# A graph layer on one core: the sums of a turn put between two first layers, and VectorE's two-input work cut into operations of 128 columns

## The chip, the cores and the metric

One core of a Trainium2 chip runs the whole layer. The metric is device time in microseconds (us), the median of three runs. "PE" is TensorE, "PEld" its weight loads, "DVE" VectorE, "ACT" ScalarE, "POOL" GpSimd and "SP" SyncE. All arithmetic is float32. The profiler writes each float32 matmul as two records, so counts of matmuls below are counts of records.

## The reference

6,250 nodes with 256 features, 206,250 edges sorted by destination, 65 numbers for each edge (the first is a polarity, the others features).

```python
h = jnp.maximum(_layernorm(x, axis=-1), 0.0)
polarity = jnp.clip(edge_attr[:, 0:1], 0.0, 1.0)
raw = edge_attr[:, 1:]
e = jax.nn.relu(raw @ W_e1.T + b_e1) @ W_e2.T + b_e2
edge_emb = (e * (polarity + 0.01)) @ W_le.T + b_le
msg = jax.nn.relu(h[src] + edge_emb)
aggr = jax.ops.segment_sum(msg, dst, num_segments=6250)
g = (h + aggr) @ W_g1.T + b_g1
gn = (g - mean(g)) * rsqrt(var(g) + 1e-5) * ln_g + ln_b
return x + jax.nn.relu(gn) @ W_g2.T + b_g2
```

W_e2 and W_le are multiplied together once (`wc_s`), so an edge costs two matrix products: the first layer (64 to 256) and the product with `wc_s` (256 to 256).

## The kernel before, in words

**Tiling.** The sorted edges are cut into blocks of 512 (four tiles of 128). Two blocks make a pair (202 pairs, index `q`); half a block, 256 edges, makes a unit (806 units, index `u`). Six blocks make a group (68 groups, index `g`); each group's sums stand in one PSUM tile `pd`, in four strips of 32 rows. 49 windows of 128 nodes finish the layer. Seven PSUM buffers `pz` go round for everything else; a new tile waits until the tile seven before it has been read.

**A unit.** `edge_part(u)` puts 8 matmul records of 256 columns on PE (L266) and one addition of 512 columns on DVE (L271), which reads PSUM and so frees the buffer. Later `whole(u)` multiplies the message by the polarity and adds the gathered rows of h (L551, two DVE operations of 256 columns, one per half of `hg[u]`, each with two tensors in SBUF and a per-row scalar), and ACT takes the maximum with 0 (L556). The rows of h are gathered by POOL, two indirect DMAs for a unit (L528), into 16 buffers `hg`. The gather for a unit is issued behind a matmul of a certain earlier unit (`last_z`) and needs a buffer that the sums have freed. `whole` trails `edge_part` by 22 units at the start and by 1 at the end.

**A turn.** Every eighth unit, for pairs 6 to 195, `turn_of` (L281) works for two pairs at once: `first_layer(q + 2)`, `first_layer(q + 3)`, then `sums`, which is `add_pairs` (L587), then the loads of two further pairs on SP. A first layer is 8 matmul records of 512 columns into four PSUM buffers (L243); ACT empties three of these (L251) and DVE one (L248). The sums are 32 records (L566), one-hot matrices `sel` by finished messages `hg`; when a group is complete ACT copies it out (L577). Engines take their instructions in the order in which this code issues them.

**What else DVE does.** `select(g)` (L536) makes the one-hot tiles of a group, one comparison of 768 columns (L541), with two tensors in SBUF. For each window `ready` (L636) multiplies and then adds statistics to the transposed x in `hT` (L639, two operations of 256 columns), and `offset` (L204) adds a bias to the rows of x (L205, 256 columns). These too read two tensors in SBUF each, and have no per-row scalar. They are called through `at(unit, fn)` and `due()` (L693): each unit takes at most one such call from the list, none in the turn's unit and the one ahead of it.

Of the kernel before, what the change touches and what calls it, by code (L numbers as in the profile page):

```python
# [17 lines left out]
P = 128  # L18
# [10 lines left out]
S = 4  # L29
L = 6  # L30
# [63 lines left out]
def gnn_kernel(ctx: ExitStack, tc: tile.TileContext, x, src_c, dst_c, dst_r, pol_c, raw_t, w_e1t, w_e2,  # L94
# [16 lines left out]

    ident = const.tile([P, P], F32, name="ident")
    eps_t = const.tile([P, 1], F32, name="eps_t")
    we1_s = const.tile([P, D], F32, name="we1_s")
    wc_s = const.tile([P, 2, D], F32, name="wc_s")
    bc_s = const.tile([P, 2, D], F32, name="bc_s")
# [27 lines left out]
    def finish_nodes(nd, ps, w, n):  # L144

        r = w * P

        def turn(a):
            pt = ps()
            for c in range(2):  # L150
                nc.tensor.transpose(pt[:, 0, c * P:c * P + n], a[:n, c * P:(c + 1) * P], ident[:n, :n])
            aT = nd.tile([P, 2, P], F32, name="aT")
            if n == P:
                nc.scalar.activation(aT, pt[:, 0, :].rearrange("p (c n) -> p c n", c=2), AF.Copy)
            else:
                for c in range(2):
                    nc.scalar.activation(aT[:, c, :n], pt[:, 0, c * P:c * P + n], AF.Copy)
            return aT

        def first(aT, bias_by_pe=False):  # L160
            ph = ps()
            if bias_by_pe:
                nc.tensor.matmul(ph[:n, 0, :], ones[0:1, :n], bg1_b[0:1], start=True, stop=False)
            for c in range(2):
                nc.tensor.matmul(ph[:n, 0, :], aT[:, c, :n], wg1_s[:, c, :], start=c == 0 and not bias_by_pe, stop=c == 1)  # L165
            hs = nd.tile([P, D], F32, name="hs")
            if bias_by_pe:
                hb = ph[:, 0, :]
            else:
                hb = hs  # L170
                nc.vector.tensor_add(hs[:n], ph[:n, 0, :], bg1_b[:n])
            mv = row_stats(nd, n, 1, lambda i: hb[:n])
            rs = nd.tile([P, 1], F32, name="rs1")
            one_over_std(rs[:n], mv, n)
            nc.vector.tensor_scalar(hs[:n], hb[:n], mv[:n, 0, 0:1], rs[:n], op0=ALU.subtract, op1=ALU.mult)
            return hs

        def second(hs):
            pt = ps()
            for c in range(2):  # L180
                nc.tensor.transpose(pt[:, 0, c * P:c * P + n], hs[:n, c * P:(c + 1) * P], ident[:n, :n])  # L181
            nT = nd.tile([P, 2, P], F32, name="nT")
            for c in range(2):
                nc.scalar.activation(nT[:, c, :n], pt[:, 0, c * P:c * P + n], AF.Relu, bias=lnb_s[:, c:c + 1],  # L184
                                     scale=lng_s[:, c:c + 1])
            return nT

        def third(nT, xt):
            po = ps()
            for c in range(2):  # L190
                nc.tensor.matmul(po[:n, 0, :], nT[:, c, :n], wg2_s[:, c, :], start=c == 0, stop=c == 1)  # L191
            ot = nd.tile([P, D], F32, name="ot")
            nc.vector.tensor_add(ot[:n], po[:n, 0, :], xt[:n])
            for i, (a, b) in enumerate(spread_out(n)):
                eng = nc.scalar if i else nc.sync
                eng.dma_start(out=out[bass.ds(r + a, b - a), :], in_=ot[a:b])

        def load_x():
            xt = nd.tile([P, D], F32, name="xt3")
            for a, b in spread_out(n):  # L200
                nc.sync.dma_start(out=xt[a:b], in_=x[bass.ds(r + a, b - a), :])
            return xt

        def offset(xt):  # L204
            nc.vector.tensor_add(xt[:n], xt[:n], bg2_b[:n])  # L205

        return turn, first, second, third, load_x, offset

# [3 lines left out]
    with fast:  # L212
# [68 lines left out]
        def turn_of(q):  # L281


            if not by_two(q):
                if q + 2 < NP:
                    first_layer(q + 2)
                sums(q == NP - 1)
                load_pair(q + 4)
            elif q % 2 == 0:
                first_layer(q + 2)  # L290
                first_layer(q + 3)
                sums(False)
                load_pair(q + 4)
                load_pair(q + 5)

# [4 lines left out]
                turn_of(u // 4)  # L300

        nc.vector.memset(eps_t, EPS)
        nc.vector.memset(ones, 1.0)
        nc.vector.memset(rs_s, 0.0)
        nc.vector.memset(nm_s, 0.0)
# [207 lines left out]
        with tc.tile_pool(name="hg", bufs=HG) as hg_p, tc.tile_pool(name="ms", bufs=5) as ms_p, \  # L513
# [21 lines left out]

            def select(g):  # L536

                n = len(blocks_of(g)) * S
                t = g * L * S
                sel[g] = sel_p.tile([P, L * S, W], F32, name="sel")  # L540
                nc.vector.tensor_tensor(  # L541
                    sel[g][:, :n, :], iota_w.rearrange("p (o w) -> p o w", o=1).to_broadcast([P, n, W]),
                    rel[:, t:t + n].rearrange("p (t o) -> p t o", o=1).to_broadcast([P, n, W]), ALU.is_equal)

            def whole(u):

                m = msg.pop(u)
                if plain(u):
                    nc.vector.tensor_add(m, m, bc_s)
                for i in range(2):  # L550
                    nc.vector.scalar_tensor_tensor(hg[u][:, i, :], m[:, i, :], pol_s[:, 2 * u + i:2 * u + i + 1],  # L551
                                                   hg[u][:, i, :], op0=ALU.mult, op1=ALU.add)
                    if u == NU - 1:
                        nc.scalar.activation(hg[u][:, i, :], hg[u][:, i, :], AF.Relu)
                if u < NU - 1:
                    nc.scalar.activation(hg[u], hg[u], AF.Relu)  # L556

            def add_up(b):

                g = group_of(b)  # L560
                k = b - g * L
                if k == 0:
                    acc[g] = pd[:, g % 2, :] if g < NG - 1 else ps()[:, 0, :]
                for j in range(S):
                    m = hg[2 * b + j // 2]
                    nc.tensor.matmul(acc[g][j * W:(j + 1) * W, :], sel[g][:, k * S + j, :], m[:, j % 2, :],  # L566
                                     start=k == 0, stop=b == blocks_of(g)[-1])
                hg.pop(2 * b)
                hg.pop(2 * b + 1)
                return g if b == blocks_of(g)[-1] else None  # L570
# [16 lines left out]
            def add_pairs(last=False):  # L587
# [3 lines left out]
                while summed < NP and min(4 * summed + 4, NU) < made + last:  # L591
                    for b in (2 * summed, 2 * summed + 1):
                        if b < NB:
                            whole_groups.append(add_up(b))
                            if b % L == 0 and group_of(b) + 2 < NG:
                                at(now + 2, lambda g=group_of(b) + 2: select(g))
                    summed += 1

                for g in whole_groups:
# [3 lines left out]
            todo = {}  # L603
            now = 0
            late = {}
            ending = {-2: [], -1: []}

            def at(u, fn):
# [2 lines left out]
            def node_work(w, spread_now=False):  # L611
# [7 lines left out]
                def spread():  # L619
# [7 lines left out]
                    for g in gs:  # L627
# [1 line left out]
                        nc.vector.tensor_scalar(s2, iota_p, rowid[:, g:g + 1], float(-w * P), op0=ALU.subtract,  # L629
                                                op1=ALU.is_equal)  # L630
                        box["sel2"].append(s2)
                    at(now + 3, lambda: ready(0))
                    at(now + 4, lambda: ready(1))
                    at(now + 5, lambda: offset(box["xt"]))

                def ready(i):  # L636

                    hT, st = box["hT"], box["st"]
                    nc.vector.tensor_tensor(hT[:, :, :n], hT[:, :, :n], st[:, i:i + 1, :n].to_broadcast([P, 2, n]),  # L639
                                            (ALU.mult, ALU.add)[i])  # L640

                def sums_of(part):

# [56 lines left out]

            gathers(HG)
            sums = add_pairs
            for i, fn in ((0, first_rows), (1, rows_of_edges), (3, lambda: select(0)), (5, row_numbers), (6, stats_out),
                          (7, lambda: select(1)), (8, node_weights)):
                at(LEAD + i, fn)
            for i, fn in enumerate((by_group(0, ALU.max), by_group(1, ALU.min), by_row(0, ALU.max), by_row(1, ALU.min),
                                    verdict, count, total)):
# [2 lines left out]
            for u in range(LEAD, NU):  # L710
# [8 lines left out]
                else:  # L719
                    gathers(4 * summed + HG - 4 + (u - TURN) % 4 + 1, last_z)  # L720

                while made < u + 1 - max(LEAST, LEAD - u // SHRINK) - (by_two(u // 4) and (u + 1) % 8 == TURN):
                    whole(made)
                    made += 1
                due()
                if u == NU - 24:
                    for w in range(NW):
                        if groups_of(w)[-1] == NG - 1:
                            late[w] = node_work(w, True)
                if u == LEAD + 60:  # L730
                    flag = nc.values_load(bad_i[0:1, 0:1], min_val=0, max_val=3 * P)
            while todo:
                now = min(todo)
                for fn in todo.pop(now):
                    fn()
            before, last = ending[-2], ending[-1]
            for sums_of, halves_out, rows_of, one, two, three, gs in before:
                rows_of()
# [28 lines left out]
def any_order(tc, dram, v):  # L767
# [7 lines left out]
    with tc.tile_pool(name="sc", bufs=1) as sc, tc.tile_pool(name="sk", bufs=2) as sk, \  # L775
# [78 lines left out]
        def nodes(w, n):  # L854
# [1 line left out]
            nc.sync.dma_start(out=ac[:n], in_=acc_d[bass.ds(w * P, n), :])  # L856
            turn, one, two, three, load_x, offset = v["finish_nodes"](sk, lambda: sp1.tile([P, 1, D], F32, name="ps_a"), w, n)
            xt = load_x()
            offset(xt)
            three(two(one(turn(ac))), xt)  # L860

        with tc.For_i(0, full, 1) as w:
# [65 lines left out]
```

## Time and profile before

| what | us |
|---|---|
| median of three runs (2186.34 to 2188.13) | 2187.48 |
| time of the profiled execution | 2189.23 |
| its span, first to last instruction | 2187.4 |
| PE busy in the span | 2169.5 |
| POOL busy | 1648.4 |
| DVE busy | 1604.4 |
| ACT busy | 960.8 |

The page of the profile gives busy time for each engine, the costliest groups of instructions by source line with the mean duration of one, and the idle time ahead of them with what ended it. A busy PE says little, since matmuls overlap and their ends are modelled. What counts is the distance from one start to the next. For POOL the page counts the indirect DMA instruction alone as busy; what lies between two of them stands as idle time. The mean granted TensorE clock was 0.997.

### The profile page before, as it was taken

To read this page: it belongs to the slowest core of one execution; us is meant where nothing else is said; L and a number is where in the kernel's file an instruction comes from. 1 tells how busy PE (TensorE), PEld (TensorE's weight loads), DVE (VectorE), ACT (ScalarE), POOL (GpSimd) and SP (SyncE) were. 2 spreads that over 40 slices of the span, in tenths; PEclk is the share of its full clock that TensorE was granted. 3 is DMA by queue.
4 is the path that set the end of the run, shared out by engine and by line. 5 is a ranking of instruction groups with operands and counts; after the bars stand their busy time and mean duration, and the time that the engine had idled before them with its cause. 6 is when DMAs were issued, how large, how long until landed. Compare 5 with 4: busy or idle time off the path is not lost.

```text
span 2187.4 us, 34907 instructions
## 1 busy us (share of the span) xinstructions
PE 2169.5 (99%) x12382; PEld 1625.1 (74%) x12382; DVE 1604.4 (73%) x3470; ACT 960.8 (44%) x1701; POOL 1648.4 (75%) x1675
## 2 busy tenths in 40 slices
PE   9999999999999999999999999999999999999998
PEld 6677777777777777777677777777777777777776
DVE  7787777777777777777677777777777767777675
ACT  7444444444444444444444444343444444444443
POOL 5777777777777777777777777777777777777775
PEclk9999999999999999999999999999999999999999
DMA  9544445454545454545544445445444445454543
GB/s 313 159 134 134 138 126 157 130 149 122 151 126 155 119 155 125 151 123 151 142 122 139 142 139 151 129 121 156 139 131 128 143 130 153 131 146 130 150 123 89
DMA packets 156075, 309.17 MB, mean 141 GB/s; under 512 B 33183, under 2 KB 77944, under 8 KB 155896
## 3 DMA queue, kind: packets, MB, share of 16 engines
q0 software_dynamic: 77376, 211.39, 33.7%
q1 hardware_dynamic: 77364, 92.23, 13.7%
q10 hardware_dynamic: 1156, 3.28, 0.4%
q8 instruction: 98, 1.61, 0.3%
q14 instruction: 81, 0.66, 0.1%
HBM read 293.92 MB, written 12.85 MB: 140 GB/s over the span
## 4 chain that ended last, share of the span: by engine, by line
PE 92%; DMA 3%; POOL 2%; DVE 2%; issue 1%; ACT 1%; ACTq 0%; DVEq 0%; POOLq 0%
PE pz L266 60%; PE pz L243 16%; PE pd L566 9%; PE pz L664 3%; DMA hg<-hb_d,src_s 3%; PE pz L165 2%; PE pz L191 2%; POOL hg L528 2%; DVE msg L271 1%; PE pz L181 1%; DMA xt<-in_x_dram 0%; ACT xt L366 0%; DVE hg L551 0%; DVE st L136 0%; PE pz L307 0%
## 5 line engine op out<-in xcount | busy, mean ns | idle before, releaser
L528 POOL DMA_INDIRECT hg<-hb_d,src_s x1612 | 1611.2, 999 | 495.5 <-issue 355.3
L266 PE MATMUL pz<-wc_s,e 128*128 128x256 f32 x6448 | 1452.3, 381 | 1.3 <-ACT msg L269 1.3
L266 PEld LDWEIGHTS pz<-wc_s,e 128*128 128x128 f32 x6448 | 1208.7, 190 | 203.8 <-issue 28.8
L556 ACT ACTIVATE hg<-hg 128x512 f32<-128x512 f32 x805 | 500.5, 629 | 1048.0 <-DVE hg L551 1030.5
L551 DVE SCALAR_TENSOR_TENSOR hg<-msg,pol_s,hg 128x256 f32<-128x256 f32 x1612 | 711.3, 478 | 153.3 <-DMA hg<-hb_d,src_s 148.9
L271 DVE TENSOR_TENSOR msg<-pz,bc_s 128x512 f32<-128x512 f32 x799 | 542.9, 685 | 224.0 <-PE pz L266 223.0
L243 PE MATMUL pz<-raw,we_s 64*128 64x512 f32 x1612 | 402.8, 608 | 6.9 <-DVE msg L271 6.6
L251 ACT ACTIVATE e<-pz,vecs 128x512 f32<-128x512 f32 x605 | 361.8, 692 | 88.0 <-PE pz L243 86.9
L243 PEld LDWEIGHTS pz<-raw,we_s 64*128 64x128 f32 x1612 | 160.2, 186 | 195.6 <-issue 127.2
L248 DVE TENSOR_SCALAR e<-pz,vecs 128x512 f32<-128x512 f32 x201 | 150.5, 749 | 164.6 <-PE pz L243 164.6
L566 PE MATMUL pd<-hg,sel 128*32 128x256 f32 x3216 | 196.9, 386 | 0.0
L566 PEld LDWEIGHTS pd<-hg,sel 128*32 128x32 f32 x3216 | 95.0, 110 | 129.3 <-issue 77.6
L664 PEld LDWEIGHTS pz<-s,ms 128*128 128x128 f32 x548 | 68.7, 192 | 3.1 <-issue 0.4
L664 PE MATMUL pz<-s,ms 128*128 128x128 f32 x548 | 69.3, 275 | 0.1
L541 DVE TENSOR_TENSOR sel<-iota_w,rel 128x768 f32<-128x768 f32 x68 | 63.9, 940 | 0.0
L370 POOL TENSOR_TENSOR hb<-xt,rows_b 128x256 f32<-128x256 f32 (+1 forms) x49 | 34.1, 728 | 24.2 <-ACT xt L366 18.2
L191 PE MATMUL pz<-wg_s,nT 128*128 128x256 f32 (+1 forms) x196 | 50.6, 380 | 0.6 <-ACT nT L184 0.6
L165 PE MATMUL pz<-wg_s,hT 128*128 128x256 f32 (+1 forms) x196 | 50.5, 380 | 0.0
L577 ACT ACTIVATE ms<-pd 128x256 f32<-128x256 f32 x66 | 25.4, 384 | 51.5 <-PE pd L566 51.5
L191 PEld LDWEIGHTS pz<-wg_s,nT 128*128 128x128 f32 (+1 forms) x196 | 37.1, 190 | 5.9 <-ACT nT L184 0.8
L165 PEld LDWEIGHTS pz<-wg_s,hT 128*128 128x128 f32 (+1 forms) x196 | 37.0, 190 | 5.7 <-issue 0.3
L639 DVE TENSOR_TENSOR hT<-hT,stb 128x256 f32<-128x256 f32 x98 | 40.8, 417 | 0.0
(90 smaller groups left out, 378.2 us busy)
## 6 DMA issues: line engine op xcount, KB each, us to landing
raw<-in_raw_t_dram SPq DMA_DIRECT2D x202, 256.0 KB
hg<-hb_d,src_s POOLq DMA_INDIRECT x1612
stb<-st_d SPq DMA_DIRECT2D x49, 128.0 KB
hb_d<-hb SPq DMA_DIRECT2D x12, 512.0 KB
xt<-in_x_dram SPq DMA_DIRECT2D x48, 128.0 KB
hT<-in_x_t_dram SPq DMA_DIRECT2D x48, 128.0 KB
out_dram<-ot SPq DMA_DIRECT2D x48, 128.0 KB
xt<-in_x_dram SPq DMA_DIRECT2D x11, 512.0 KB
```

Of the source, the lines that this page charges most:

```text
L165: nc.tensor.matmul(ph[:n, 0, :], aT[:, c, :n], wg1_s[:, c, :], start=c == 0 and not bias_by_pe, stop=c == 1)
L191: nc.tensor.matmul(po[:n, 0, :], nT[:, c, :n], wg2_s[:, c, :], start=c == 0, stop=c == 1)
L243: nc.tensor.matmul(pe[s, c], we1_s[s * F:(s + 1) * F, c * P:(c + 1) * P], raw[q][s * F:(s + 1) * F, :], start=True, stop=True)
L248: nc.vector.tensor_scalar(e1[b][:, c, :], pe[s, c], be1_s[:, c:c + 1], 0.0, op0=ALU.add, op1=ALU.max)
L251: nc.scalar.activation(e1[b][:, c, :], pe[s, c], AF.Relu, bias=be1_s[:, c:c + 1])
L266: last_z = nc.tensor.matmul(pz[:, i, :], e1[b][:, c, k:k + P], wc_s[:, c, :], start=c == 0, stop=c == 1)
L271: nc.vector.tensor_add(msg[u], pz, bc_s)
L528: g = nc.gpsimd.indirect_dma_start(out=hg[u][:, i, :], out_offset=None, in_=hb_d, in_offset=bass.IndirectOffsetOnAxis(ap=src_s[:, 2 * u + ...
L551: nc.vector.scalar_tensor_tensor(hg[u][:, i, :], m[:, i, :], pol_s[:, 2 * u + i:2 * u + i + 1], hg[u][:, i, :], op0=ALU.mult, op1=ALU.add)
L556: nc.scalar.activation(hg[u], hg[u], AF.Relu)
L566: nc.tensor.matmul(acc[g][j * W:(j + 1) * W, :], sel[g][:, k * S + j, :], m[:, j % 2, :], start=k == 0, stop=b == blocks_of(g)[-1])
L664: nc.tensor.matmul(pa[:, c, :n], ms[g][:, c * P:(c + 1) * P], box["sel2"][i][:, :n], start=i == 0, stop=i == len(gs) - 1)
```

## The change

It does four things. The sums of a turn are issued between its two first layers. Each product of `whole` is issued as two operations of 128 columns. The one-hot comparison is issued block by block (six pieces of 128 columns), and `ready` and `offset` in halves of 128 columns; these become `scalar_tensor_tensor` with a per-row scalar `zero_c` that is added first (a column of zeros, written once at the start). And they no longer go through `due()`: `piece()` issues one of them in each unit ahead of the products, those of a window first (`steps`), otherwise the next one-hot piece (`rest`), and a second one when more than six one-hot pieces are left. Before a group's first sums, pieces of that group still left would be issued at once.

```diff
@@ turn_of
             elif q % 2 == 0:
                 first_layer(q + 2)
+                sums(False)
                 first_layer(q + 3)
-                sums(False)
                 load_pair(q + 4)
                 load_pair(q + 5)
@@ offset
-        def offset(xt):
-            nc.vector.tensor_add(xt[:n], xt[:n], bg2_b[:n])
+        def offset(xt, c):
+            h = slice(c * P, (c + 1) * P)
+            nc.vector.scalar_tensor_tensor(xt[:n, h], xt[:n, h], zero_c[:n], bg2_b[:n, h], op0=ALU.add, op1=ALU.add)
@@ select
-                n = len(blocks_of(g)) * S
-                t = g * L * S
-                sel[g] = sel_p.tile([P, L * S, W], F32, name="sel")
-                nc.vector.tensor_tensor(
-                    sel[g][:, :n, :], iota_w.rearrange("p (o w) -> p o w", o=1).to_broadcast([P, n, W]),
-                    rel[:, t:t + n].rearrange("p (t o) -> p t o", o=1).to_broadcast([P, n, W]), ALU.is_equal)
+                return [(g, lambda k=k: rows_of_block(g, k)) for k in range(len(blocks_of(g)))]
+
+            def rows_of_block(g, k):
+                t = (g * L + k) * S
+                if k == 0:
+                    sel[g] = sel_p.tile([P, L * S, W], F32, name="sel")
+                nc.vector.scalar_tensor_tensor(
+                    sel[g][:, k * S:(k + 1) * S, :], iota_w.rearrange("p (o w) -> p o w", o=1).to_broadcast([P, S, W]),
+                    zero_c, rel[:, t:t + S].rearrange("p (t o) -> p t o", o=1).to_broadcast([P, S, W]), op0=ALU.add,
+                    op1=ALU.is_equal)
+
+            def piece():
+                if steps and steps[0][0] <= now:
+                    steps.popleft()[1]()
+                elif rest:
+                    rest.popleft()[1]()
@@ whole
                 for i in range(2):
-                    nc.vector.scalar_tensor_tensor(hg[u][:, i, :], m[:, i, :], pol_s[:, 2 * u + i:2 * u + i + 1],
-                                                   hg[u][:, i, :], op0=ALU.mult, op1=ALU.add)
+                    for c in range(2):
+                        h = slice(c * P, (c + 1) * P)
+                        nc.vector.scalar_tensor_tensor(hg[u][:, i, h], m[:, i, h], pol_s[:, 2 * u + i:2 * u + i + 1],
+                                                       hg[u][:, i, h], op0=ALU.mult, op1=ALU.add)
@@ add_up, add_pairs
+                    while rest and rest[0][0] <= g:
+                        rest.popleft()[1]()
...
-                                at(now + 2, lambda g=group_of(b) + 2: select(g))
+                                rest.extend(select(group_of(b) + 2))
@@ node_work
-                    at(now + 3, lambda: ready(0))
-                    at(now + 4, lambda: ready(1))
-                    at(now + 5, lambda: offset(box["xt"]))
+                    steps.extend((now + 3, lambda i=i, c=c: ready(i, c)) for i in range(2) for c in range(2))
+                    steps.extend((now + 3, lambda c=c: offset(box["xt"], c)) for c in range(2))
...
-                def ready(i):
+                def ready(i, c):
-                    nc.vector.tensor_tensor(hT[:, :, :n], hT[:, :, :n], st[:, i:i + 1, :n].to_broadcast([P, 2, n]),
-                                            (ALU.mult, ALU.add)[i])
+                    nc.vector.scalar_tensor_tensor(hT[:, c, :n], hT[:, c, :n], zero_c, st[:, i, :n], op0=ALU.add,
+                                                   op1=(ALU.mult, ALU.add)[i])
@@ main loop
+                piece()
                 while made < u + 1 - max(LEAST, LEAD - u // SHRINK) - (by_two(u // 4) and (u + 1) % 8 == TURN):
                     whole(made)
                     made += 1
                 due()
+                if len(rest) > 6:
+                    piece()
```

More of the change, by code (lines that the diff above doesn't have):

```diff
@@ L113, in gnn_kernel @@
     eps_t = const.tile([P, 1], F32, name="eps_t")
+    zero_c = const.tile([P, 1], F32, name="zero_c")
     we1_s = const.tile([P, D], F32, name="we1_s")
@@ L302, in gnn_kernel @@
         nc.vector.memset(eps_t, EPS)
+        nc.vector.memset(zero_c, 0.0)
         nc.vector.memset(ones, 1.0)
@@ L605, in gnn_kernel @@
             late = {}
+            steps = deque()
+            rest = deque()
             ending = {-2: [], -1: []}
@@ L702, in gnn_kernel @@
             sums = add_pairs
-            for i, fn in ((0, first_rows), (1, rows_of_edges), (3, lambda: select(0)), (5, row_numbers), (6, stats_out),
-                          (7, lambda: select(1)), (8, node_weights)):
+            for i, fn in ((0, first_rows), (1, rows_of_edges), (3, lambda: rest.extend(select(0) + select(1))), (5, row_numbers), (6, stats_out),
+                          (8, node_weights)):
                 at(LEAD + i, fn)
@@ L735, in gnn_kernel @@
                     fn()
+            while steps:
+                steps.popleft()[1]()
             before, last = ending[-2], ending[-1]
@@ L858, in nodes @@
             xt = load_x()
-            offset(xt)
+            offset(xt, 0)
+            offset(xt, 1)
             three(two(one(turn(ac))), xt)
```

## The prediction

> **What bounds the kernel now.** The page comes first, and it points at PE. So does the chain of waits (92% PE).
>
> ```profile
> PE 2169.5 (99%) x12382; PEld 1625.1 (74%) x12382; DVE 1604.4 (73%) x3470; ACT 960.8 (44%) x1701; POOL 1648.4 (75%) x1675
> ...
> L528 POOL DMA_INDIRECT hg<-hb_d,src_s x1612 | 1611.2, 999 | 495.5 <-issue 355.3
> L266 PE MATMUL pz<-wc_s,e 128*128 128x256 f32 x6448 | 1452.3, 381 | 1.3 <-ACT msg L269 1.3
> ```
>
> But POOL's 75% is misread: between gathers stands a constant. The view by source line gives their range, the waits their gaps.
>
> ```profile
> L528 POOL DMA_INDIRECT hg<-hb_d,src_s x1612: 940/947/2088, 64.5 to 2168.0; - x180
> ```
>
> ```profile
> POOL hg L528 <- issue: 355.3, 1163, 0.9
> ...
> DVE hg L551 <- DMA hg<-hb_d,src_s: 148.9, 199, 2.8
> ...
> PEld pz L243 <- DVE msg L271: 41.1, 81, 3.1
> ```
>
> 355.3/1163 is 0.306 us. Going through the 1611 gaps one by one, all but 7 are 0.303 to 0.306 whatever releaser is named. So a gather costs 0.305 + its duration, and 1612 × (0.305 + 0.999) = 2102 us fill the stretch from 64.5 to 2169 (2104): POOL issues without a pause from the first gather to the last. DVE then waits for rows that land late (148.9 us), L271 queued behind frees PSUM late, and PE stands in the first layer (41.1). A turn with such a wait and one without, in the timeline (start, duration):
>
> ```profile
> 1014.55 4.83 PE L243 MATMUL pz<-raw,we_s 64*128 64x512 f32 x16
> ...
> 1017.40 0.29 PEld L243 LDWEIGHTS pz<-raw,we_s 64*128 64x128 f32 x2 [0.84 <-DVE msg L271]
> ```
>
> ```profile
> 1036.53 3.70 PE L243 MATMUL pz<-raw,we_s 64*128 64x512 f32 x16
> ...
> 1038.66 0.75 DVE L248 TENSOR_SCALAR e<-pz,vecs 128x512 f32<-128x512 f32 x1 [1.33 <-PE pz L243]
> ...
> 1040.31 0.75 DVE L248 TENSOR_SCALAR e<-pz,vecs 128x512 f32<-128x512 f32 x1 [0.89 <-PE pz L243]
> 1040.98 1.66 DVE L551 SCALAR_TENSOR_TENSOR hg<-msg,pol_s,hg 128x256 f32<-128x256 f32 x4
> ```
>
> **PE's own floor.** From first L243 start to first L566 start, 94 turns take 375.0 us in sum and 3.63 at the shortest: 375.0 − 341.2 = 33.8 of waiting. The same count over sums and products gives 4.6 more. So PE has only 38 us of stalls; without them the span is 2149.
>
> **What stretches a gather.** A clean one takes 0.945. All of the excess sits beside DVE operations with two tensors in SBUF:
>
> ```profile
> 1007.42 0.95 DVE L541 TENSOR_TENSOR sel<-iota_w,rel 128x768 f32<-128x768 f32 x1
> ...
> 1007.74 1.46 POOL L528 DMA_INDIRECT hg<-hb_d,src_s  x1 [0.30 <-PE pz L266]
> ```
>
> Here DVE ends at 1008.37 and the gather at 1009.20, 0.83 later. Record by record, a lengthened gather ends 0.82 after the DVE operation that ran 0.125 into it. Sorted by that operation: L551 37.6 us (291 gathers, worst 0.33), L541 26.1 (56), L639 11.4 (33), L205 7.9 (18), together 83.0. If gathers arrive at any moment, a hold of h costs h²/(2 × 1.305) for each operation; 37.6 us over 1612 gives h = 0.247, and 0.247/1.305 × 1612 = 305 gathers, near the 291. The hold is about the time of 256 columns, not the whole 0.478. And a gather held by L551 is let through ahead of another L551, but when L541, L639 or L205 follows it is held through that one too: these have no per-row scalar.
>
> **The change, part by part.**
>
> *POOL.* The price of a column is (0.868 − 0.335)/512 = 1.04 ns, from the steps (end to end, back to back) of L541 and L639 behind L551; 128 columns are 0.133. So h becomes 0.247 − 0.133 = 0.114. There are 3224 products, 403 one-hot pieces, 196 + 98 halves: 3921 × 0.114²/2.61 = 19.5 us for 83.0, a gain of 63. Bounds: a hold that stays 0.247 gives 91.6 (9 worse), none at all a gain of 83. I take 63, as the hold follows the columns. The stream would end near 2187 − 63 = 2124, before PE's floor: POOL stops being the bound and would next wait for PE, behind whose matmuls its gathers are issued.
>
> *DVE pays.* Four L551 in a row take 1.66 and two 0.87, a step of 0.396. A step of 128 columns isn't in the trace with two tensors: below stands L629's 0.195 (128 columns, one tensor), above the full duration 0.478 − 0.133 = 0.343. I take 0.396 − 0.133 = 0.263, the same form with fewer columns. Products: 806 × (4 × 0.263 − 2 × 0.396) = 209 us. One-hot: 403 × 0.263 − 68 × 0.868 = 47. h and x: 294 × 0.263 − 147 × 0.335 = 28. Together 284: DVE busy 1604 → 1888. Is there cover? A turn comes every 21.46 us (mean of starts), with 8.2 units; the window from 400 to 2000 has 1173.17 of 1600 us busy, or 15.7 per turn. It becomes 15.7 + 2.9 = 18.6, plus 1.5 of waiting for gathers: 20.1 of the 21.3 that a turn would last (21.46 − 38/95 + 0.21, the last term from the next part). It hides in DVE's waits for PE (L271 223.0, L248 164.6). Without that cover it costs up to 2.9 per turn, 275 us.
>
> *The sums between.* They move ahead of 8 records on PE, L577 ahead of three L251 on ACT; SP and POOL are not passed. First layer then products takes 1.92 (6 cases near the ends), two then sums 3.63, sums then products 1.86. Before: 3.63 + 1.86 = 5.49; after: 1.92 + 1.86 + 1.92 = 5.70, one more refilling of PE. 0.21 × 95 = 20 us on PE's path; bounds 0 (the sums refill for nothing) to 0.4 (twice that), 0 to 38 us. The second L248 becomes ready some 5.9 into the turn, not 3.8. Behind it in DVE's queue stand the products of two units and a piece; L271 of the next unit follows, 5.9 + 0.66 + 8 × 0.263 + 0.26 = 8.9 into the turn, where PE has finished at 5.7 + 1.8 = 7.5, and six other PSUM buffers cover that. L577 waits until 3.8, but the first of its three L251 is ready only at 4.3. The sums come 1.7 earlier; their last products were issued three units before, so their messages are ready. In exchange the second first layer asks for buffers 1.9 later, which takes most waits as in the 4.83 turn away.
>
> *The order of pieces.* 697 pieces over 784 units, one for each, so none is forced ahead of sums; it costs nothing beyond the above. Windows' other steps lose the five list entries ahead of them and come a unit or so sooner, their five DMA issues on SP too; SP has room.
>
> **Sum.** 2187.4 − 38 (stalls) + 20 (refilling) + 4 (a tenth of the stalls stays) = 2173 of span. Around the span lie 1.8 us (2189.23), and the median of the runs is 1.75 below that execution, so 2173 for the median as well. Own range: 2149 (free refilling, no stall) to 2187 (0.4 a turn).
>
> **The rivals.**
>
> *Slower, DVE becomes the bound.* A turn leaves 21.3 − 20.1 = 1.2 us. Each turn has 33 products and 7 pieces, so it tips from a step of 0.263 + 1.2/40 = 0.29. At 0.30 the turn needs 20.1 + 40 × 0.037 = 21.6, and waits in order at L248 that can't all be filled (0.2 or so) bring 21.8: (21.8 − 21.46) × 95 = +32, 2220. At 0.343 it is 23.3, +175. For it: the queue is in order, and the second L248 holds DVE longer. Against: steps of the same form are steady (0.393 to 0.397 for four in five), and shorter gather waits give part back.
>
> *No change, POOL stays the bound.* If a hold lasted as long as its instruction, cutting would gain nothing: L551 37.6 × 2 × (0.343/0.478)² = 38.7, L541 26.1 × 6 × (0.343/0.950)² = 20.4, L639 and L205 19.3 × 2 × (0.343/0.417)² = 26.1, together 85 for 83. PE's 20 would go into its stalls: 2189. For it: blocks do end with the DVE operation. Against: 0.33 as the worst wait beside L551. The Trainium skill, "SBUF — State Buffer", section Who interferes with whom, has this rule: a VectorE instruction with two SBUF inputs and a GpSimd one that reads SBUF share a port pair, held for the whole instruction. That they block each other the trace confirms; that it is the whole instruction it doesn't, for 0.478 would have cost 1612 × 0.478²/2.61 = 141 us where 37.6 stand.
>
> **Chances.** Forecast 0.62, DVE bound 0.25, no change 0.13. What a measurement can tell from nothing is 0.2%, 2183 to 2192. Of the forecast 0.58 lies below it, 0.03 in it, 0.01 above; of no change 0.02, 0.09 and 0.02; DVE bound is all above. Faster 0.60, same 0.12, slower 0.28. The range 2150 to 2212 leaves out the worse half of DVE bound and little else.
>
> **What would show it.** Mean L528 near 0.957 with L551's worst wait under 0.2; POOL gaps above 0.31 by the hundred; DVE busy near 1888 and L551 steps of 0.263; first layer, sums, first layer, products at 1.92 + 1.86 + 1.92 with hardly a wait on L271. It is wrong if DVE's waits for PE vanish and L243 waits for L271 grow, or if L528's mean stays at 0.999.

## The result and the profile after

The changed kernel takes 2246.89 us (median of 6 runs, 2243.04 to 2255.49) against 2187.41 for the one before (6 runs, 2186.11 to 2189.05): a ratio of 1.0276, with a 95% interval of 1.0258 to 1.0293. It is slower by 2.8%, where 2173 us had been forecast, and lies above the forecast's range. The profiled execution is the longest of the six (2255.49 us, span 2253.7, clock 0.993), so what is counted in it comes out up to 9 us larger than in the median run.

The page of the changed kernel, the line of engines and two groups (products are now L568, gathers L531):

```profile
PE 2223.0 (99%) x12382; PEld 1629.7 (72%) x12382; DVE 1864.3 (83%) x5565; ACT 965.3 (43%) x1701; POOL 1715.5 (76%) x1675
...
L531 POOL DMA_INDIRECT hg<-hb_d,src_s x1612 | 1678.2, 1041 | 494.6 <-issue 351.0
...
L568 DVE SCALAR_TENSOR_TENSOR hg<-msg,pol_s,hg 128x128 f32<-128x128 f32 x3224 | 923.6, 343 | 183.9 <-DMA hg<-hb_d,src_s 179.1
```

Its gathers by source line, with the shortest, the median and the longest in ns and the first and the last start:

```profile
L531 POOL DMA_INDIRECT hg<-hb_d,src_s x1612: 942/949/2507, 63.9 to 2233.6; - x180
```

Its waits (total us, times, longest):

```profile
POOL hg L531 <- issue: 351.0, 1147, 1.5
DVE hg L568 <- DMA hg<-hb_d,src_s: 179.1, 237, 2.7
...
PEld pz L245 <- DVE msg L273: 65.7, 107, 2.4
...
DVE msg L273 <- PE pz L268: 7.4, 10, 2.8
```

Read the gather row first. The mean went from 0.999 to 1.041 us while the median stayed at 0.949: a minority became much longer. The gaps are the constant they were (351.0/1147 is 0.306, and only 2 of the 1611 exceed 0.31). So POOL still issues without a pause, and 1612 × 0.042 = 67 us is the whole growth of the span (66.3 from profile to profile). The rest follows down the chain that the waits showed before: DVE waits longer for rows (148.9 to 179.1), the additions that free PSUM come later, and PE's wait for them grows from 41.1 to 65.7. DVE itself has no time left for PE at these additions: that wait was 223.0 and is 7.4. Measured from start to start on PE, the first layers of the turns stood 65 us above the 1.92 that each takes without a wait.

To see what made gathers long, each lengthened one was put down to the DVE operation that ended 0.82 us ahead of its end, as in the kernel before. The excess over 0.945:

| operation | before, us (gathers) | after, us (gathers) |
|---|---|---|
| products | 37.6 (291) | 129.0 (480) |
| one-hot | 26.1 (56) | 4.9 (34) |
| h, `ready` | 11.4 (33) | 4.0 (26) |
| x, `offset` | 7.9 (18) | 2.1 (10) |

The pieces went the way that was forecast of them, 45.4 us going down to 11.0. The products went the other way. Their long waits stand in the timeline, here POOL and then DVE over the same stretch (start, duration; "x4" is four operations in a row):

```profile
1075.86 1.61 POOL L531 DMA_INDIRECT hg<-hb_d,src_s  x1 [0.30 <-issue]
1077.77 1.61 POOL L531 DMA_INDIRECT hg<-hb_d,src_s  x1 [0.30 <-issue]
1079.68 1.61 POOL L531 DMA_INDIRECT hg<-hb_d,src_s  x1 [0.30 <-issue]
```

```profile
1076.56 0.69 DVE L273 TENSOR_TENSOR msg<-pz,bc_s 128x512 f32<-128x512 f32 x1
1077.16 0.35 DVE L207 SCALAR_TENSOR_TENSOR xt<-xt,zero_c,rows_b 128x128 f32<-128x128 f32 x1
1077.42 1.14 DVE L568 SCALAR_TENSOR_TENSOR hg<-msg,pol_s,hg 128x128 f32<-128x128 f32 x4
1078.47 0.69 DVE L273 TENSOR_TENSOR msg<-pz,bc_s 128x512 f32<-128x512 f32 x1
1079.07 0.35 DVE L207 SCALAR_TENSOR_TENSOR xt<-xt,zero_c,rows_b 128x128 f32<-128x128 f32 x1
1079.33 1.14 DVE L568 SCALAR_TENSOR_TENSOR hg<-msg,pol_s,hg 128x128 f32<-128x128 f32 x4
```

Take the gather of 1077.77. At 0.125 into it, 1077.90, the second of four products runs (they start at 1077.42, 1077.68, 1077.95 and 1078.21). It isn't let through behind the second, nor behind the third: it ends at 1079.38, 0.82 after the end of the fourth (1078.56). That is 0.66 above a clean gather, 0.13 for the rest of the second product and two steps of 0.263. In all, 103 gathers were held from the second product to the end of the fourth (67.5 us) and 63 from the third (25.5 us). These **joined holds**, which go on from one operation into the next, make 93 of the 129 us.

The stretch shows one thing more: the three gathers start 1.91 apart, and so do DVE's units (1077.42, 1079.33). When a gather is released at the end of a unit's products, the next one reaches the point where it can be held 1.25 us (0.82 + 0.305 + 0.125) later, and with 0.66 of waiting that is one unit of DVE. So it falls on the same spot of the next unit again: 39 of the 103 were followed at once by another such gather.

### The profile page after: what moved, and what is told of

It reads as the page before. It is cut to its first block, busy times and chain, and to the rows that moved or that the text cites. A ratio compares the mean times of both kernels' runs of the same rounds, so it can differ in the third digit from the quotient of the medians.

```text
span 2253.7 us, 38221 instructions
## 1 busy us (share of the span) xinstructions
PE 2223.0 (99%) x12382; PEld 1629.7 (72%) x12382; DVE 1864.3 (83%) x5565; ACT 965.3 (43%) x1701; POOL 1715.5 (76%) x1675
## 5 line engine op out<-in xcount | busy, mean ns | idle before, releaser
L531 POOL DMA_INDIRECT hg<-hb_d,src_s x1612 | 1678.2, 1041 | 494.6 <-issue 351.0
L568 DVE SCALAR_TENSOR_TENSOR hg<-msg,pol_s,hg 128x128 f32<-128x128 f32 x3224 | 923.6, 343 | 183.9 <-DMA hg<-hb_d,src_s 179.1
L573 ACT ACTIVATE hg<-hg 128x512 f32<-128x512 f32 x805 | 507.3, 630 | 1196.8 <-DVE hg L568 1096.8
L245 PE MATMUL pz<-raw,we_s 64*128 64x512 f32 x1612 | 453.6, 622 | 15.1 <-DVE msg L273 14.5
L253 ACT ACTIVATE e<-pz,vecs 128x512 f32<-128x512 f32 x605 | 370.5, 690 | 49.7 <-PE pz L245 49.1
L250 DVE TENSOR_SCALAR e<-pz,vecs 128x512 f32<-128x512 f32 x201 | 149.5, 744 | 157.1 <-PE pz L245 155.9
L548 DVE SCALAR_TENSOR_TENSOR sel<-iota_w,zero_c,rel 128x128 f32<-128x128 f32 x403 | 136.9, 340 | 0.0
L659 DVE SCALAR_TENSOR_TENSOR hT<-hT,zero_c,stb 128x128 f32<-128x128 f32 (+1 forms) x196 | 66.6, 340 | 0.0
L185 ACT ACTIVATE nT<-pz,vecs 128x128 f32<-128x128 f32 (+1 forms) x98 | 38.7, 445 | 2.4 <-PE pz L182 2.4
```

The source lines that it names most:

```text
L245: nc.tensor.matmul(pe[s, c], we1_s[s * F:(s + 1) * F, c * P:(c + 1) * P], raw[q][s * F:(s + 1) * F, :], start=True, stop=True)
L250: nc.vector.tensor_scalar(e1[b][:, c, :], pe[s, c], be1_s[:, c:c + 1], 0.0, op0=ALU.add, op1=ALU.max)
L253: nc.scalar.activation(e1[b][:, c, :], pe[s, c], AF.Relu, bias=be1_s[:, c:c + 1])
L531: g = nc.gpsimd.indirect_dma_start(out=hg[u][:, i, :], out_offset=None, in_=hb_d, in_offset=bass.IndirectOffsetOnAxis(ap=src_s[:, 2 * u + ...
L548: nc.vector.scalar_tensor_tensor(sel[g][:, k * S:(k + 1) * S, :], iota_w.rearrange("p (o w) -> p o w", o=1).to_broadcast([P, S, W]), zero_ ...
L568: nc.vector.scalar_tensor_tensor(hg[u][:, i, h], m[:, i, h], pol_s[:, 2 * u + i:2 * u + i + 1], hg[u][:, i, h], op0=ALU.mult, op1=ALU.add)
```

## The experiments

Three theories came first. A: POOL's stream stays the bound, and the products of 128 columns lengthen it. B: DVE's added work is the bound, in its in-order queue. C: the moved sums or the pieces cost the time.

**The first four runs** took one part each, or left one out. `sums_only` is the kernel before with this edit alone:

```diff
                 first_layer(q + 2)
+                sums(False)
                 first_layer(q + 3)
-                sums(False)
```

`split_only` is the kernel before with the products in two operations of 128 columns:

```diff
-                    nc.vector.scalar_tensor_tensor(hg[u][:, i, :], m[:, i, :], ...)
+                    for c in range(2):
+                        h = slice(c * P, (c + 1) * P)
+                        nc.vector.scalar_tensor_tensor(hg[u][:, i, h], m[:, i, h], ...)
```

`pieces_only` is the kernel before with one-hot, h and x in operations of 128 columns behind `zero_c`, called through `piece()`, as in the diff further up. `after_256` is the changed kernel with the products back at 256 columns.

> The kernel before with the sums of a turn between its two first layers, nothing else. Theory A (POOL's stream of gathers is the bound before and after, and the loss comes from the products of 128 columns, which lengthen the gathers): gathers stay at a mean of 0.999 us, the refilling of PE (20 us) goes into stalls of PE that are there anyway, 2187 us give or take 6. Theory B (DVE's added work is the bound): the same, DVE's work is unchanged. Theory C (the moved sums cost PE or ACT): 2220 or more.

> The kernel before with each product as two operations of 128 columns, nothing else. Theory A: gathers lengthen by as much as in the changed kernel or more (there 155 us of excess over 0.945 for 88), mean 1.04 us, 2250 us. Theory B (DVE busy 1604 + 209 = 1813): between the two kernels, about 2235, with the mean gather following rather than leading and POOL pausing now and then. Theory C: 2187.

> The kernel before with the one-hot in pieces and h and x in halves behind adds, products of 256 columns, sums after both first layers. Theory A: the 45 us beside L541, L639 and L205 fall to some 10, gathers at a mean of 0.978 us, 2155 us. Theory B (DVE busy 1604 + 75 = 1679): a little slower than before, 2195. Theory C (the pieces cost, by their order ahead of the products): 2200 or more.

> The changed kernel with products of 256 columns again, all else as changed. Theory A: gathers at a mean of 0.978 us, PE with few stalls but 20 us more of refilling, 2150 to 2170 us, faster than both kernels. Theory B: 2195. Theory C: 2230 or more.

When these four ran, the kernel before took 2592.42 us itself, 405 more than otherwise. The four measured 2614.41, 2619.04, 2612.18 and 2611.85, ratios of 1.0103 [1.0058, 1.0149], 1.0113 [1.008, 1.0147], 1.0088 [1.0055, 1.0121] and 1.0104 [1.006, 1.0149]. None tells a theory from another: all are 1% slower, and their intervals overlap. What differs there is waiting. The gather group of `sums_only` at that time, and of the same kernel (`sums_only_2`) at the next occasion:

```profile
L528 POOL DMA_INDIRECT hg<-hb_d,src_s x1612 | 1653.6, 1026 | 861.0 <-issue 546.7
```

```profile
L528 POOL DMA_INDIRECT hg<-hb_d,src_s x1612 | 1613.1, 1001 | 492.9 <-issue 360.1
```

The idle time ahead of gathers is 368 us larger, while the gather itself is 0.025 longer. POOL pauses there, so it isn't the bound, and a time from then says little on a kernel that POOL bounds in the others. What such traces do show is how each gather fared beside DVE: mean gathers of 1.026, 1.055, 0.995 and 0.987 in the order above, so the split stood out already.

**The same four again**, at an occasion when the kernel before took 2185.75 (15 runs):

> The kernel before with each product as two operations of 128 columns, once more: the first four runs fell on a chip where the kernel before itself takes 2592 us, POOL pauses for some 400 us and engines wait several us for each other's signals, so they can't decide between theories on a kernel of 2187 us. Where before takes 2187: theory A (POOL's gathers, lengthened by the products, are the bound) mean gather 1.04 or more, 2250 us; theory B (DVE's work) about 2235 with pauses of POOL; theory C (the sums or the pieces cost) 2187.

> The changed kernel with products of 256 columns, once more for the same reason. Theory A: gathers at a mean of 0.978 us, 2150 to 2170 us. Theory B: 2195. Theory C: 2230 or more.

> The kernel before with one-hot in pieces and h and x in halves behind adds, nothing else, once more. Theory A: mean gather 0.978, 2155 us. Theory B: 2195. Theory C: 2200 or more.

> The kernel before with the sums between the first layers, nothing else, once more. Theories A and B: mean gather 0.999, 2187 us give or take 6. Theory C: 2220 or more.

| kernel | us | ratio, 95% interval | mean gather, us |
|---|---|---|---|
| split_only_2 | 2236.57 | 1.0224 [1.0207, 1.0241] | 1.031 |
| after_256_2 | 2178.99 | 0.9967 [0.9955, 0.998] | 0.985 |
| pieces_only_2 | 2170.88 | 0.993 [0.9913, 0.9946] | 0.979 |
| sums_only_2 | 2187.26 | 1.0006 [0.9996, 1.0015] | 1.001 |

The split alone costs 2.2%; the changed kernel without it is 0.3% faster than the one before, and the pieces alone are 0.7% faster. C falls: the moved sums change nothing by themselves. The pages of `split_only_2`, `after_256_2` and `pieces_only_2`:

```profile
PE 2201.1 (98%) x12382; PEld 1634.6 (73%) x12382; DVE 1803.1 (81%) x5082; ACT 963.4 (43%) x1701; POOL 1698.8 (76%) x1675
...
L528 POOL DMA_INDIRECT hg<-hb_d,src_s x1612 | 1661.5, 1031 | 495.7 <-issue 354.5
```

```profile
PE 2165.3 (99%) x12382; PEld 1609.3 (74%) x12382; DVE 1660.3 (76%) x3953; ACT 983.0 (45%) x1701; POOL 1625.7 (75%) x1675
...
L531 POOL DMA_INDIRECT hg<-hb_d,src_s x1612 | 1588.4, 985 | 507.3 <-issue 350.0
```

```profile
PE 2154.5 (99%) x12382; PEld 1616.1 (74%) x12382; DVE 1678.2 (77%) x3953; ACT 963.8 (44%) x1701; POOL 1615.6 (74%) x1675
...
L531 POOL DMA_INDIRECT hg<-hb_d,src_s x1612 | 1578.4, 979 | 507.5 <-issue 362.0
```

In `split_only_2` the idle time of POOL is the constant (1611 × 0.305 is 491; the rest lies ahead of the first gather and in a handful of gaps), and gathers and gaps fill the stretch from the first gather to the last, as before. In the other two 30 gaps exceed 0.31, by 14 us in sum over the constant: the gathers are short enough that POOL begins to wait. But A and B aren't told apart yet: where the gather is long, DVE also has more work (1803 against 1660 and 1678).

`split_only_2` shows besides where its gathers lose: those that met a product and went on into further operations have an excess of 86 us, 26 of it up to the end of a later product and 60 up to the end of a one-hot, h or x operation behind the products. In the kernel before, 26 us stood there, all of it with those three.

**Theories of the hold.** Going through the traces record by record, each held gather (0.025 us or more above a clean one) was sorted by the place of the operation it met, the one running 0.125 into it, in an unbroken run of operations with two SBUF inputs. It was counted how often the hold went on into the next operation of the run:

| trace | first or second of a run | third | fourth |
|---|---|---|---|
| changed kernel | 1 of 128 | 115 of 189 | 38 of 61 |
| split_only_2 | 0 of 87 | 122 of 172 | 21 of 31 |
| after_256_2 (products of 256) | 2 of 129 | 1 of 24 | 1 of 9 |
| pieces_only_2 (products of 256) | 0 of 206 | 0 of 12 | 1 of 16 |

(Only cases with a next operation count.) A piece ahead of the products is the first of their run, so the second product of such a unit stands third; in `split_only_2`, which has no pieces, it is the third product, and no gather was held on from the second. That gave theory D: from the third of an unbroken run of 128-column operations on, holds join. E and F were rivals on the hold itself, that it is as long for 128 columns as for 256 in any order, or that it hangs on whether the next product has another scalar. `after_breaks` is the changed kernel with a one-column memset on DVE ahead of a unit's products and between the first two and the last two, which leaves no run longer than two:

```diff
+                nc.vector.memset(gap_c, 0.0)
                 for i in range(2):
+                    if i:
+                        nc.vector.memset(gap_c, 0.0)
                     for c in range(2):
```

`after_256_load` has products of 256 columns, and more work on DVE without a second SBUF input:

```diff
-                nc.vector.tensor_add(msg[u], pz, bc_s)
+                nc.vector.tensor_add(msg[u][:, 0, :], pz[:, 0, :], bc_s[:, 0, :])
+                for c in range(2):
+                    h = slice(c * P, (c + 1) * P)
+                    nc.vector.tensor_add(msg[u][:, 1, h], pz[:, 1, h], bc_s[:, 1, h])
```

`after_cmajor` is the changed kernel with the two loops over i and c exchanged, so that neighbouring products have different scalars. `pieces_split_breaks` is `after_breaks` with the sums behind both first layers, as in the kernel before.

> The changed kernel with two more DVE instructions in each unit, a memset of one column ahead of the products and one between the first and the last two of them; nothing else. Theory D (from the third of an unbroken run of two-input operations of 128 columns on, the holds join, and a gather that meets one waits for the whole rest of the run; the memsets leave no run longer than two): the excess beside the products falls from 129 us to some 35, mean gather 0.98, and the time to 2175 to 2195 us, though DVE has about 100 us more to do. Theory B (DVE's work is the bound): 2290 or more. Theory E (128 columns hold as long as 256 do, in whatever order): no change, 2247.

> The changed kernel with products of 256 columns, and L273, which reads PSUM and only one tensor in SBUF, in three operations of 256, 128 and 128 columns: 806 x 2 x 0.131 = 211 us more for DVE, as much as the split products brought (DVE busy about 1870), without another hold on POOL. Theory A and D: gathers stay at 0.985, and the time near the 2179 of the kernel with 256 columns, up to 2190. Theory B: as slow as the changed kernel, 2247.

> The changed kernel with the four products of a unit in another order: first half of both gathered tiles, then second half of both, so that the per-row scalar and the tile change from each to the next. Theory D (the place in the run decides): as the changed kernel, 2247, mean gather 1.04. Theory F (the holds join where the scalar changes, between the second and the third product, or where it stays, between the third and the fourth): they join at other places, and the excess beside the products moves by half or more, to under 90 or over 180 us; 2210 or 2290.

> As the first kernel of these four, with the sums after both first layers again, which spares the 20 us of refilling. Theory D: mean gather 0.98, 2160 to 2175, near the 2171 of the kernel with the pieces alone; if the products' excess falls below the 42 us that it has there, under 2165. Theory B: 2290. Theory E: 2235.

This occasion was like the first (the kernel before: 2546.51), and the times, 2609.58, 2607.37, 2600.46 and 2649.36, with ratios of 1.0238 [1.0203, 1.0274], 1.0248 [1.0189, 1.0308], 1.0195 [1.0158, 1.0232] and 1.0406 [1.0364, 1.0447], missed what was expected and decide nothing. The page of `after_breaks` shows what kind of waiting it is:

```profile
L251 DVE TENSOR_SCALAR e<-pz,vecs 128x512 f32<-128x512 f32 x201 | 149.8, 745 | 464.4 <-remote 171.5
```

"remote" is a wait put down to something outside what the trace records; on the changed kernel this row's idle time is 157.1, of which 155.9 for PE. The gathers speak nonetheless. With the breaks no gather was held over from one product to the next, the worst hold by a product fell from 0.66 (two were longer) to 0.152, and the mean gather to 0.972. In c-major order the holds joined as before, 158 of 196 at the third place of a run and 1 of 143 at the first two: 135 gathers from the second product to the end of the fourth, 88.0 us, at a mean gather of 1.059. So the scalar has no part in it (F falls), and a single hold of 128 columns is short (E falls).

**Three of them again**, with the kernel before at 2187.63 (25 runs):

> The changed kernel with a one-column memset on VectorE ahead of a unit's products and another between the first two and the last two of them: 1612 more instructions on VectorE (about 48 us busy), and no run of more than two back-to-back operations with two SBUF inputs. D (joined holds are what lengthens the gathers): no gather over 0.945 + 0.16 us behind products, mean gather 0.97 to 0.98, no longer a stream of POOL that sets the end (1612 x (0.305 + 0.975) = 2063), PE's floor 2149 + about 20 of refilling: 2165 to 2190 us. B (VectorE's work is the bound): at or above the 2247 of the changed kernel, 2247 to 2300. A third: the memsets hold or delay as much as they save, 2200 to 2247.

> The changed kernel with products of 256 columns, and with the bias addition that follows the second layer made in three operations (256, 128, 128 columns) out of PSUM: about 85 to 210 us more work on VectorE than with products of 256 columns alone (2179 us), with no second SBUF input. D: VectorE's work costs nothing as such, 2177 to 2195 us. B: as VectorE's work comes back to that of the changed kernel, so does its time, 2220 to 2260 us.

> As after_breaks_2, but with the sums of a turn behind both first layers, as in the kernel before. D: the refilling of PE between first layers (about 8 us on top of the pieces) is gone, and with gathers of 0.97 to 0.98 us the floor of PE is reached as by the pieces alone (2170.9 us) or somewhat closer: 2155 to 2175 us. B: 2230 to 2290, as the split alone (2236.6) or above.

| kernel | us | ratio, 95% interval | mean gather, us | DVE busy, us |
|---|---|---|---|---|
| after_breaks_2 | 2186.25 | 0.9994 [0.9984, 1.0003] | 0.970 | 1864.7 |
| after_256_load_2 | 2182.97 | 0.9979 [0.997, 0.9989] | 0.993 | 1751.6 |
| pieces_split_breaks_2 | 2187.19 | 0.9997 [0.9987, 1.0006] | 0.972 | 1884.1 |

`after_breaks_2` decides between A with D and B. Its page, and its one wait of products for rows:

```profile
PE 2172.7 (99%) x12382; PEld 1610.2 (74%) x12382; DVE 1864.7 (85%) x7177; ACT 975.3 (45%) x1701; POOL 1600.3 (73%) x1675
...
L532 POOL DMA_INDIRECT hg<-hb_d,src_s x1612 | 1563.0, 970 | 535.4 <-issue 388.0
...
L572 DVE SCALAR_TENSOR_TENSOR hg<-msg,pol_s,hg 128x128 f32<-128x128 f32 x3224 | 920.0, 344 | 6.5 <-DMA hg<-hb_d,src_s 5.8
```

```profile
DVE hg L572 <- DMA hg<-hb_d,src_s: 5.8, 10, 1.2
```

DVE is as busy as in the changed kernel (1864.7 and 1864.3 us) and has 1612 instructions more, and yet the kernel is 61 us faster. What went is the joined holds: of the gathers that met a second or third product, 166 of 312 were held to the end of the fourth in the changed kernel, and here none of 101. The products' wait for rows falls from 179.1 to 5.8. Two gathers of it, POOL and then DVE:

```profile
1100.68 1.10 POOL L532 DMA_INDIRECT hg<-hb_d,src_s  x1 [0.30 <-issue]
1102.08 1.08 POOL L532 DMA_INDIRECT hg<-hb_d,src_s  x1 [0.30 <-issue]
```

```profile
1100.07 0.34 DVE L549 SCALAR_TENSOR_TENSOR sel<-iota_w,zero_c,rel 128x128 f32<-128x128 f32 x1
1100.34 0.34 DVE L572 SCALAR_TENSOR_TENSOR hg<-msg,pol_s,hg 128x128 f32<-128x128 f32 x1
1100.36 0.06 DVE L566 MEMSET gap_c<- 128x1 f32 x1
1100.60 0.62 DVE L572 SCALAR_TENSOR_TENSOR hg<-msg,pol_s,hg 128x128 f32<-128x128 f32 x2
1100.89 0.06 DVE L569 MEMSET gap_c<- 128x1 f32 x1
1101.14 0.34 DVE L572 SCALAR_TENSOR_TENSOR hg<-msg,pol_s,hg 128x128 f32<-128x128 f32 x1
1101.40 0.68 DVE L274 TENSOR_TENSOR msg<-pz,bc_s 128x512 f32<-128x512 f32 x1
1102.00 0.34 DVE L549 SCALAR_TENSOR_TENSOR sel<-iota_w,zero_c,rel 128x128 f32<-128x128 f32 x1
```

The gather of 1100.68 meets the second product (1100.60 to 1100.94; in the program the memset of 1100.89 stands behind it) and ends at 1101.78, 0.83 after it, although the third and the fourth follow without a pause. In the changed kernel such a gather waits for the end of the fourth in 103 cases of 210. Nor is it another beat: a unit with a piece takes 1.93 here (1100.07 to 1102.00) and 1.91 above. `after_256_load_2` agrees from the other side:

```profile
PE 2169.3 (99%) x12382; PEld 1608.8 (74%) x12382; DVE 1751.6 (80%) x5551; ACT 977.9 (45%) x1701; POOL 1638.6 (75%) x1675
```

91 us more on DVE than in `after_256_2` cost 4 us (3 by the ratios). That is less than half of the 204 that the split brings, and of the 211 first expected of this edit, so it is the weaker of the two tests. B falls as the cause of the loss.

`pieces_split_breaks_2` missed: 2155 to 2175 was expected and 2187.19 measured, 16 us above `pieces_only_2`, with gathers even shorter (0.972 against 0.979) and 64 pauses of POOL. On PE the stretch from first layer to sums takes 374.4 us where it takes 359.8 there, so the difference stands in PE's waits, and POOL isn't its cause. DVE has 206 us more to do. PE's waits in the first layers don't settle how that costs time. For the additions they are little longer than in `pieces_only_2`, for ACT's emptying of the buffers more so (this kernel first):

```profile
PEld pz L246 <- DVE msg L274: 28.4, 48, 3.9
PEld pz L246 <- ACT e L254: 14.1, 36, 1.3
```

```profile
PEld pz L245 <- DVE msg L273: 26.4, 62, 2.5
PEld pz L245 <- ACT e L253: 4.1, 10, 1.3
```

The cause of these 16 us stays open.

The best kernel here is `pieces_only_2`, with 2170.88 us ahead of both; it needs only the pieces.

## Why the prediction was wrong

**The step that failed** is the price of the products within "So h becomes 0.247 − 0.133 = 0.114 ... 3921 × 0.114²/2.61 = 19.5 us for 83.0". The products' part of these 19.5 is 3224 × 0.114²/2.61 = 16 us. They measured 129. The formula takes each operation alone, and it rests on the sentence that a gather held by L551 "is let through ahead of another L551". That was true of 256 columns and was carried to 128, where no row of the trace showed it. At the third and fourth operation of a run it fails in some 60% of the cases. Where no holds join, the price of the products is near: in `after_breaks_2` they measure 17.6 us (270 gathers, worst 0.151). The upper bound, "a hold that stays 0.247 gives 91.6 (9 worse)", was no bound either, since it too lets a gather through behind every operation; the loss was 67. The step on the order of pieces, "it costs nothing beyond the above", fell with it: a piece ahead of the products makes their run longer by one, and lets a gather that meets the second product be held on.

**The rest, step by step.** That POOL's stream bounds the kernel was right, and it is why the failed price went straight into the time. The 45.4 us of one-hot, h and x fell to 11.0, where the formula gives them 697 × 0.114²/2.61 = 3.5; without joined holds of products (`pieces_only_2`) they measure 8.2, so this term was too small as well. DVE's step was 0.263 as forecast and its busy time 1864, 1888 being forecast. The sums between cost the refilling as priced: where PE doesn't wait, the three parts of a turn take 1.92, 1.86 and 1.92. With the split undone (`after_256_2`) the kernel took 2178.99, 8 us above the pieces with the sums behind, which refill less but wait more.

**DVE's cover** was nearly what it had been called. With joined holds gone, 204 us of added DVE work cost 7 us (2178.99 to 2186.25, or 6 by the ratios), which stand as waits in first layers: from start to start those of the turns add to 391.1 us in `after_breaks_2` and 384.3 in `after_256_2`. So 2173 would have been some 13 us low even without the joined holds.

**The rivals.** DVE as the bound was forecast at 2220 and gave the right sign by the wrong mechanism: it needed a step of 0.29 or more, and the step stayed at 0.263. The sign that the prediction named for being wrong, DVE's waits for PE vanishing and the first layer's waits for additions growing, came true in part, but didn't tell the mechanisms apart. DVE's wait for first layers in the changed kernel, then the waits of `after_breaks_2` for first layers and at the additions, and PE's there for the additions:

```profile
DVE e L250 <- PE pz L245: 155.9, 104, 5.8
```

```profile
DVE e L251 <- PE pz L246: 258.1, 131, 6.9
DVE msg L274 <- PE pz L269: 15.5, 16, 2.8
```

```profile
PEld pz L246 <- DVE msg L274: 18.3, 47, 2.3
```

DVE's wait at the additions, 223.0 before and 7.4 in the changed kernel, is only 15.5 in `after_breaks_2`, where rows no longer come late. So it wasn't the joined holds that took it away, and its loss cost little. PE's wait for the additions, 65.7 in the changed kernel, is 18.3 there: that one had grown with the joined holds.

"No change" came closer in kind: POOL's stream stayed the bound. It let a hold cover the whole instruction. The Trainium skill ("SBUF — State Buffer", section Who interferes with whom) says that a VectorE instruction with two SBUF inputs contends with a GpSimd one that reads SBUF, and, of VectorE's two-port modes, that the shared pair is held for the whole instruction. By this trace the whole instruction is both too long and too short: a lone operation of 0.344 holds a gather for 0.15 at most, and operations in a row hold it beyond the end of the one that it met, up to 0.66.

**What stays open** is why the first two operations of a run let a gather through and the later ones often don't, and why only some 60% of the later ones hold on. Nor is the place in the run an exact rule: at the fifth place only 2 of 25 went on in the changed kernel and 0 of 11 in `split_only_2`, and farther on it was 29 of 45 and 5 of 17. What in the hardware makes holds join, no run here shows.

## What to carry to other kernels

When GpSimd's stream of gathers is the bound, price an edit on VectorE by what it does to the gathers, and take the price from runs of operations as the new kernel will issue them, not from one operation alone. Shorter operations with two SBUF inputs helped at the head of a run and in pairs (one-hot, h and x: 45 us to 11; products between memsets: 37.6 to 17.6) and hurt in unbroken runs of four and more. A busy time that hasn't changed can still stretch another engine's instructions: compare the mean with the median of the row that bounds, then look for what ends together with the long ones.

## What the hardware showed beyond that

- A one-column memset (0.06 us, and hardly 0.01 of VectorE's time each by the beat of 1.93 against 1.91) between two operations lets a waiting gather through: with two in each unit, the usual longest hold by products fell from 0.66 to 0.15.
- In a stretch where neither GpSimd nor VectorE shows a wait for the other, the two fell into step through such holds: three gathers 1.91 us apart, in the beat of VectorE's units, each held at the same product.
- On two of five occasions the kernel before took 2592 and 2547 us instead of 2187, with VectorE's instructions at their usual length (a product 0.344, an addition 0.681), the granted clock at 0.952 in `after_breaks` (0.993 in the changed kernel's profile) and the loss in waits, some marked "remote". There an edit of 2.2% measured 1.1%, and one of −0.7% measured +0.9%. What made those two different wasn't found; the record names chip 1 both for the 2592 and for the 2186 of the next occasion.
